# Experts' stage: PE in written order, sum products two chunks later, end and survey of a group in parts

## The chip, the cores and the metric

The kernel runs on one core of a Trainium2 chip. The metric is the device time of one execution in microseconds; lower is better. Five engines work side by side: TensorE (PE, with its weight loads shown apart as PEld), VectorE (DVE), ScalarE (ACT), GpSimd (POOL) and SyncE (SP, which here only issues transfers). Everything is computed in float32.

## The reference

Two layers work on 8192 tokens (32 sequences of 256) of width 128, each a residual step on a layer norm:

```
x = x + causal_attention(layernorm(x))          # 16 heads
x = x + experts(layernorm(x))                   # this case
x = x + hyperbolic_attention(layernorm(x))      # 16 heads, arccosh distances
x = x + feed_forward(layernorm(x))              # 128 -> 512 -> 128
```

The experts' step, cut to its core:

```
topk_idx, topk_weight = gate(x)                 # sigmoid scores, best 2 of 4 groups, best 4 of 16 experts
g = einsum('th,eih->eti', x, gate_proj)         # 16 experts, inner width 64
u = einsum('th,eih->eti', x, up_proj)
expert_out = einsum('eti,ehi->eth', silu(g) * u, down_proj)
y = sum over the 4 chosen experts of topk_weight * expert_out
y = y + (silu(x @ shared_gate.T) * (x @ shared_up.T)) @ shared_down.T
```

## The kernel before

The tokens are cut into 16 groups of 512 (`NG`, `GT`); x of all groups stays on the chip in `self.xg`. The stages follow one another: causal attention, experts, a test of a flag on the chip, and then one of two versions of the second attention with the feed-forward step (here the far one, `far_attention`).

Every expert is computed for every token, and the routing weight, zero for those not chosen, is multiplied in. Two experts of inner width 64 make a chunk of 128 rows, so there are 8 chunks and, as ninth, the shared expert (64 rows): `NCH = 8`. In `experts` the loop goes over groups, and in it over the nine chunks. One chunk is:

- PE: `g_ps` (L696) and `u_ps` (L698), weights times the 512 normed tokens `bxT`;
- ACT: `act`, the Silu of `g_ps` (L700);
- DVE: `act` times `u_ps` (L701), and but for the shared expert times the routing weights `wb` (L703);
- PE: `y_ps`, added up over the nine chunks (L704).

At chunk 1 `fetched` (L671, L677) issues on SP the transfers of the next group's tokens and routing weights. At the end of a group ACT copies the sum to `yT` (L708), and `add_transposed` turns it back with four PE transposes (L109) and adds it to x on DVE (L110).

Then `survey` prepares the second attention for the group: DVE's statistics (L612, L613), POOL's `sxn`, x less its mean (L614), four PE transposes into `xc_ps` (L620), ACT's copy `sxc` (L622), an SP write of it to memory (L623), twice two products `sqk` with the query and key weights (L628), ACT's squares (L633), DVE's sums (L634), and on DVE the end: least and greatest norm, and `ra` (L637 to L642). `survey_result` makes the flag from all groups' ends.

Beside this the routing of the last four groups (12 to 15) is still to be computed: `preparation` returns 26 pieces. In order they are four statistics, deviations, for each group normed (POOL `rxn`, L504), tokens (PE transposes L511) and scored (PE `logits` L520), then `best_groups` (DVE, L541 to L559), and for each group `weights` (DVE comparisons, L533 to L538, and L569 to L574) and `turned` (PE transposes `wT_ps`, L579, and a write to memory). One piece is written out after each odd chunk. The fetch of group 12, at group 11, reads what they write.

No order is fixed by hand in this stage: a planner goes over the program when it is built, with estimated costs, and puts each engine's instructions in a fixed order, by readiness and the order in which they were written. It may take a later one first. In the causal attention before it, `tc.manual_schedule(engines={mybir.EngineType.PE})` keeps PE in the written order while the planner orders the others. [...] `act` has three buffers.

Of the kernel before, what the change touches and what calls it, by code (L numbers as in the profile page):

```python
# [9 lines left out]
F32 = mybir.dt.float32  # L10
BF16 = mybir.dt.bfloat16
AF = mybir.ActivationFunctionType
ALU = mybir.AluOpType
AX = mybir.AxisListType
PSUM = bass.MemoryType.PSUM

P = 128
B, N, D = 32, 256, 128
T = B * N
TG = 4  # L20
GT = TG * P
NG = T // GT
QUAD = 4
EPS = 1e-5

H = 16
DH = D // H
# [4 lines left out]
NE, INTER = 16, 64  # L32
# [8 lines left out]
class Net:  # L41
# [562 lines left out]

    def survey(self, pool, psum, g):

        nc = self.nc
        mv = pool.tile([P, TG, 2], F32, tag="smv", name=f"smv{g}")
        xn = pool.tile([P, TG, D], F32, tag="sxn", bufs=1, name=f"sxn{g}")
        for t in range(TG):  # L610
            st = pool.tile([P, nc.vector.BN_STATS_DIM], F32, tag="sst", bufs=4, name=f"sst{g}_{t}")
            nc.vector.bn_stats(st, self.xg[g][:, t, :])  # L612
            nc.vector.bn_aggr(mv[:, t, :], st)  # L613
            nc.gpsimd.tensor_scalar(xn[:, t, :], self.xg[g][:, t, :], mv[:, t, 0:1], None, ALU.subtract)  # L614
        rv = self.rv[:, g]
        nc.vector.tensor_scalar(rv, mv[:, :, 1], EPS, None, ALU.add)
        nc.vector.reciprocal(rv, rv)
        ps = psum.tile([P, GT], F32, tag="w", name=f"xc_ps{g}")
        for t in range(TG):
            nc.tensor.transpose(ps[:, t * P : (t + 1) * P], xn[:, t, :], self.ident)  # L620
        xc = pool.tile([P, GT], F32, tag="sxc", name=f"sxc{g}")
        nc.scalar.copy(xc, ps)  # L622
        nc.sync.dma_start(out=self.xc[g], in_=xc)  # L623
        n2 = pool.tile([P, TG, 2 * H], F32, tag="sn2", name=f"sn2_{g}")
        for i in range(2):
            qk = psum.tile([P, 2, 2 * D], F32, tag="w", name=f"sqk{g}_{i}")
            for t in range(2):
                nc.tensor.matmul(  # L628
                    qk[:, t], xc[:, (2 * i + t) * P : (2 * i + t + 1) * P], self.w_qkv[:, 0 : 2 * D],
                    start=True, stop=True,  # L630
                )
            sq = pool.tile([P, 2, 2 * D], F32, tag="ssq", bufs=1, name=f"ssq{g}_{i}")
            nc.scalar.activation(sq, qk, AF.Square)  # L633
            nc.vector.tensor_reduce(  # L634
                n2[:, 2 * i : 2 * i + 2], sq.rearrange("p t (h d) -> p t h d", d=DH), AX.X, ALU.add
            )
        nc.vector.tensor_mul(n2, n2, rv.unsqueeze(2).to_broadcast([P, TG, 2 * H]))  # L637
        nc.vector.tensor_reduce(self.ends[:, 0, g : g + 1], n2, AX.XY, ALU.min)
        nc.vector.tensor_reduce(self.ends[:, 1, g : g + 1], n2, AX.XY, ALU.max)
        ra = self.ra[:, g].rearrange("p t s h -> p t (s h)")  # L640
        nc.vector.tensor_scalar(ra, n2, -1.0, 1.0, ALU.mult, ALU.add)
        nc.vector.reciprocal(ra, ra)  # L642

    def survey_result(self, pool, psum):

# [12 lines left out]
    def experts(self, prep):  # L658
        nc, tc = self.nc, self.tc
        NCH = NE * INTER // P  # L660
        w_g, w_u, w_d, s_g, s_u, s_d = (self.w_e[n] for n in ("w_g", "w_u", "w_d", "s_g", "s_u", "s_d"))
        with (
            tc.tile_pool(name="mo", bufs=2) as pool,
            tc.tile_pool(name="mops", bufs=2, space=PSUM) as psum,
        ):

            def fetched(g):


                xT = pool.tile([P, GT], F32, tag="xT", bufs=3, name=f"bxT{g}")  # L670
                nc.sync.dma_start(out=xT, in_=self.xt[g])  # L671
                wb = pool.tile([P, NCH, GT], F32, tag="wb", bufs=3, name=f"wb{g}")
                rows = self.rows[g].rearrange("(c e) t -> e c t", e=2)
                for c in range(0, NCH, 1 if g == 0 else NCH):
                    cs = slice(c, c + 1 if g == 0 else NCH)
                    for e in range(2):
                        nc.sync.dma_start(  # L677
                            out=wb[e * INTER : (e + 1) * INTER, cs], in_=rows[e, cs].partition_broadcast(INTER)
                        )
                return xT, wb  # L680

            pieces = self.preparation(NG // QUAD - 1, prep, psum, "w")
            ready = fetched(0)
            for g in range(NG):
                xT, wb = ready
                y_ps = psum.tile([P, GT], F32, tag="y", name=f"y_ps{g}")
                for c in range(NCH + 1):
                    if c == 1 and g + 1 < NG:
                        ready = fetched(g + 1)
                    shared = c == NCH  # L690
                    m = INTER if shared else P
                    wg = s_g if shared else w_g[:, c * P : (c + 1) * P]
                    wu = s_u if shared else w_u[:, c * P : (c + 1) * P]
                    wd = s_d if shared else w_d[:, c, :]
                    g_ps = psum.tile([P, GT], F32, tag="g", name=f"g_ps{g}_{c}")
                    nc.tensor.matmul(g_ps[:m, :], wg, xT, start=True, stop=True)  # L696
                    u_ps = psum.tile([P, GT], F32, tag="u", name=f"u_ps{g}_{c}")
                    nc.tensor.matmul(u_ps[:m, :], wu, xT, start=True, stop=True)  # L698
                    act = pool.tile([P, GT], F32, tag="act", bufs=3, name=f"act{g}_{c}")
                    nc.scalar.activation(act[:m, :], g_ps[:m, :], AF.Silu)  # L700
                    nc.vector.tensor_mul(act[:m, :], u_ps[:m, :], act[:m, :])  # L701
                    if not shared:
                        nc.vector.tensor_mul(act, act, wb[:, c])  # L703
                    nc.tensor.matmul(y_ps, wd, act[:m, :], start=c == 0, stop=shared)  # L704
                    if c % 2 == 1 and pieces:
                        pieces.pop(0)()
                yT = pool.tile([P, GT], F32, tag="yT", name=f"yT{g}")
                nc.scalar.copy(yT, y_ps)  # L708
                self.add_transposed(pool, psum, "u", g, yT)
                self.survey(pool, psum, g)  # L710
            self.survey_result(pool, psum)


# [785 lines left out]
```

## Time and profile before

| what | value |
|---|---|
| median of 3 runs | 2361.95 us (2359.27 to 2363.54) |
| the profiled execution | 2362.43 us, its span 2360.5 us |
| PE busy | 2084.4 us, 88% of the span |
| DVE busy | 1569.7 us, 67% |
| ACT busy | 1391.4 us, 59% |
| POOL busy | 736.7 us, 31% |
| experts' stage, first g_ps to last yT | 1040.62 to 1507.08 us |
| from there to the flag | 1521.65 us |

Times in the profile are microseconds from the start of the span. A line of a timeline gives start, duration, engine, line of the kernel, operation, what is written and read with its shape, the number of instructions merged, and in brackets the engine's idle time before it with what ended it. The product of 128x512 in float32 is two passes on PE and shows as x2. PE's passes overlap, and their ends are modelled, so lengths are read from start to start.

### The profile page before, as it was taken

Reading aid. Unit: us, or ns where it says so; the run is one execution under the profiler, and the core shown is the slowest. Engines: PE = TensorE matmul, PEld = TensorE weight load, DVE = VectorE, ACT = ScalarE, POOL = GpSimd, SP = SyncE. Lnnn points to the kernel's source line nnn. Section 1 sums busy time; section 2 is a strip of 40 time slices with the busy share of each in tenths; the row PEclk is TensorE's granted clock in tenths of the full one; section 3 lists DMA queues with packets and bytes.
Section 4 is the critical chain, followed back from the end, with each engine's and each line's share of the span. In section 5 each row is a group of like instructions: output and inputs, shape, how many; then the busy total and the mean of one; then the engine's idle time right before and its main releaser. Section 6 shows DMA issues by size and latency. Waiting matters only on the chain.

```text
span 2360.5 us, 38340 instructions
## 1 busy us (share of the span) xinstructions
PE 2084.4 (88%) x14083; PEld 1320.4 (56%) x14083; DVE 1569.7 (67%) x4820; ACT 1391.4 (59%) x2429; POOL 736.7 (31%) x809
## 2 busy tenths in 40 slices
PE   5999999999999999979999999766787787787877
PEld 4777777777777777744443333344444444444443
DVE  2656666587658765765695555457777777777774
ACT  1776677666766676632222222267767777777774
POOL 3000001100010001002110000157777777777773
PEclk9999999999999999989999999878989999999999
DMA  4000000000000000036444332000000000000000
GB/s 145 1 1 2 1 1 6 10 7 3 1 15 6 3 1 14 7 85 135 98 91 90 89 90 49 27 5 5 10 10 14 10 10 14 10 14 10 10 5 20
DMA packets 43940, 66.65 MB, mean 28 GB/s; under 512 B 3616, under 2 KB 16688, under 8 KB 43744
## 3 DMA queue, kind: packets, MB, share of 16 engines
q1 hardware_dynamic: 40960, 59.00, 10.3%
q0 software_dynamic: 1200, 3.78, 0.5%
q8 instruction: 114, 1.87, 0.3%
q10 hardware_dynamic: 1584, 1.34, 0.2%
q14 instruction: 82, 0.67, 0.1%
HBM read 50.99 MB, written 13.11 MB: 27 GB/s over the span
## 4 chain that ended last, share of the span: by engine, by line
PE 57%; DVE 16%; POOL 10%; ACT 8%; issue 6%; DMA 1%; POOLq 0%; ACTq 0%; DVEq 0%; SPq 0%
PE t_ps L258 9%; PE s L286 9%; POOL fv L1192 8%; DVE fv L1184 6%; PE y_ps L704 5%; ACT ft L1177 5%; PE s L279 4%; PE g_ps L696 4%; PE fs L1123 4%; PE av L335 4%; PE u_ps L698 3%; PE pa_ps L316 2%; DVE fxn L1219 2%; PE pb_ps L322 2%; PE pa_ps L315 2%
## 5 line engine op out<-in xcount | busy, mean ns | idle before, releaser
L1192 POOL TENSOR_TENSOR fv<-ft,fv 128x512 f32<-128x512 f32 x480 | 567.4, 1214 | 197.2 <-ACT fv L1187 168.0
L273 DVE CUSTOM_DVE_ANT_0 p<-s,mask 128x128 f32<-128x128 f32 (+1 forms) x1024 | 316.0, 353 | 297.5 <-PE s L279 175.9
L301 ACT ACTIVATE p<-p,lo 128x128 f32<-128x128 f32 (+1 forms) x1024 | 373.7, 444 | 162.9 <-DVE lo L295 162.6
L1184 DVE SCALAR_TENSOR_TENSOR fv<-fs,ft 128x1024 f32<-128x1024 f32 x256 | 301.4, 1219 | 94.7 <-ACT ft L1177 67.8
L1177 ACT ACTIVATE ft<-fs 128x1024 f32<-128x1024 f32 x256 | 248.1, 1021 | 179.6 <-PE fs L1123 169.1
L1123 PE MATMUL fs<-fqT,fkT 32*128 32x256 f32 x2048 | 162.7, 435 | 133.7 <-DVE fv L1184 133.5
L286 PE MATMUL s<-xT,tT 128*128 128x256 f32 x1024 | 266.8, 383 | 9.0 <-DVE lo L273 9.0
L258 PE MATMUL t_ps<-xT,m_all 128*128 128x512 f32 x512 | 252.6, 613 | 3.3 <-ACT score L525 1.9
L1187 ACT ACTIVATE fv<-fv 128x2048 f32<-128x2048 f32 x128 | 246.9, 1929 | 0.0
L700 ACT ACTIVATE act<-g_ps 128x512 f32<-128x512 f32 x144 | 85.9, 596 | 232.4 <-PE g_ps L696 216.1
L1123 PEld LDWEIGHTS fs<-fqT,fkT 32*128 32x128 f32 x2048 | 103.1, 201 | 200.3 <-DVE fv L1184 111.7
L216 POOL TENSOR_TENSOR x<-x,w_bp 128x512 f32<-128x512 f32 x16 | 21.6, 1348 | 613.7 <-DVE xn L213 613.7
L286 PEld LDWEIGHTS s<-xT,tT 128*128 128x128 f32 x1024 | 177.7, 194 | 25.2 <-DVE lo L273 11.6
L259 ACT ACTIVATE tT<-t_ps,m_bias 128x512 f32<-128x512 f32 x256 | 161.0, 672 | 21.0 <-PE t_ps L258 20.6
L504 POOL TENSOR_SCALAR rxn<-x,rmv,rrstd 128x128 f32<-128x128 f32 x64 | 51.2, 811 | 377.3 <-PE rxT_ps L511 223.2
L279 PEld LDWEIGHTS s<-xT,tT 128*128 128x128 f32 x1024 | 134.3, 192 | 60.3 <-issue 56.9
L614 POOL TENSOR_SCALAR sxn<-x,smv 128x128 f32<-128x128 f32 x64 | 44.8, 716 | 384.2 <-DVE smv L613 287.5
L701 DVE TENSOR_TENSOR act<-u_ps,act 128x512 f32<-128x512 f32 x144 | 97.7, 680 | 96.7 <-PE u_ps L698 88.5
L1135 PE MATMUL fav<-fv,fva 128*32 128x257 f32 x2048 | 149.8, 408 | 7.0 <-ACT fqT L1329 2.1
L696 PE MATMUL g_ps<-bxT,w_w_g 128*128 128x512 f32 x256 | 132.9, 604 | 3.1 <-DMA bxT<-xt 3.1
L704 PE MATMUL y_ps<-act,w_w_d 128*128 128x512 f32 x256 | 134.0, 615 | 1.4 <-DVE act L703 0.5
L279 PE MATMUL s<-xT,tT 128*128 128x128 f32 x1024 | 134.9, 275 | 0.0
(223 smaller groups left out, 3736.5 us busy)
## 6 DMA issues: line engine op xcount, KB each, us to landing
wb<-rows SPq DMA_DIRECT2D x30, 1024.0 KB, 8.0
xt<-rxT SPq DMA_DIRECT2D x16, 256.0 KB, 2.0
bxT<-xt SPq DMA_DIRECT2D x16, 256.0 KB, 7.6
xc<-sxc SPq DMA_DIRECT2D x16, 256.0 KB, 2.1
fxc<-xc SPq DMA_DIRECT2D x16, 256.0 KB, 2.6
out<-x SPq DMA_DIRECT2D x16, 256.0 KB, 2.3
x<-in_x SPq DMA_DIRECT2D x8, 256.0 KB, 10.7
x<-in_x POOLq DMA_DIRECT2D x8, 256.0 KB, 10.4
```

What stands on the lines that cost most here:

```text
L258: nc.tensor.matmul(ps, m_all[:, h], G["xT"], start=True, stop=True)
L273: nc.vector.tensor_tensor_reduce(out=out, in0=x, in1=m, scale=-scale, scalar=3e38, op0=ALU.add, op1=ALU.min, accum_out=accum)
L279: nc.tensor.matmul(s0[:, j], tT[:, j, o : o + P], xT[:, o : o + P], start=True, stop=True)
L286: nc.tensor.matmul(s[:, l], tT[:, j + l, o + P : o + N], xT[:, o : o + N], start=True, stop=True)
L301: nc.scalar.activation(p[:, l], p[:, l], AF.Exp, bias=lo[:, c, l : l + 1], scale=-1.0)
L696: nc.tensor.matmul(g_ps[:m, :], wg, xT, start=True, stop=True)
L704: nc.tensor.matmul(y_ps, wd, act[:m, :], start=c == 0, stop=shared)
L1123: nc.tensor.matmul(sc[:, j, kc], kT[rows, kc * P : (kc + 1) * P], qT[rows], start=True, stop=True)
L1177: nc.scalar.activation(t[:, i : i + 2], sc[:, i : i + 2], AF.Relu, scale=-4.0)
L1184: nc.vector.scalar_tensor_tensor(v[:, x, :, 0:N], sc[:, x], 0.5, t[:, x], ALU.subtract, ALU.mult)
L1187: nc.scalar.activation(v[:, :, :, 0:N], v[:, :, :, 0:N], AF.Sqrt, scale=-4.0)
L1192: eng.tensor_sub(v[:, j, :, 0:N], t[:, j], v[:, j, :, 0:N])
```

## The change

PE keeps the written order in the experts' stage. A chunk is now a function `hidden` that issues `g_ps`, `u_ps`, Silu and the products on DVE and returns `add`, which issues the chunk's `y_ps` and, for the shared expert, the copy to `yT`. The loop holds two such functions back, so `y_ps` of chunk c is written after `g_ps` and `u_ps` of chunk c + 2; those of the last two chunks follow chunks 0 and 1 of the next group. `act` has four buffers.

`survey` returns five parts and `finish` puts `add_transposed` ahead of the first. They are written in the next group: yT's transposes, addition, statistics and sxn after chunk 2, the transposes into `xc_ps` after chunk 4, the products `sqk` after chunks 5 and 6, the end after chunk 7. The routing pieces come after chunks 1, 3 and 8: three to a group, where there were four. `add_transposed` takes a bank of tag `w`, where it took `u`. After the last group everything that is left follows at once.

```
     def survey(self, pool, psum, g):
...
+        def centred():
+            mv = pool.tile([P, TG, 2], F32, tag="smv", name=f"smv{g}")
...
+        def turned():
+            ps = psum.tile([P, GT], F32, tag="w", name=f"xc_ps{g}")
+            for t in range(TG):
+                nc.tensor.transpose(ps[:, t * P : (t + 1) * P], made["xn"][:, t, :], self.ident)
+            xc = made["xc"] = pool.tile([P, GT], F32, tag="sxc", name=f"sxc{g}")
+            nc.scalar.copy(xc, ps)
+            nc.sync.dma_start(out=self.xc[g], in_=xc)
+
+        def product(i):
...
+        def ends():
...
+        return [centred, turned, lambda: product(0), lambda: product(1), ends]
...
+            def hidden(g, c, xT, wb):
+
+                shared = c == NCH
...
+                g_ps = psum.tile([P, GT], F32, tag="g", name=f"g_ps{g}_{c}")
+                nc.tensor.matmul(g_ps[:m, :], wg, xT, start=True, stop=True)
+                u_ps = psum.tile([P, GT], F32, tag="u", name=f"u_ps{g}_{c}")
+                nc.tensor.matmul(u_ps[:m, :], wu, xT, start=True, stop=True)
+                act = pool.tile([P, GT], F32, tag="act", bufs=4, name=f"act{g}_{c}")
+                nc.scalar.activation(act[:m, :], g_ps[:m, :], AF.Silu)
+                nc.vector.tensor_mul(act[:m, :], u_ps[:m, :], act[:m, :])
+                if not shared:
+                    nc.vector.tensor_mul(act, act, wb[:, c])
+
+                def add():
+                    if c == 0:
+                        sums[g] = psum.tile([P, GT], F32, tag="y", name=f"y_ps{g}")
+                    nc.tensor.matmul(sums[g], wd, act[:m, :], start=c == 0, stop=shared)
+                    if shared:
+                        yT = sums[g, "T"] = pool.tile([P, GT], F32, tag="yT", name=f"yT{g}")
+                        nc.scalar.copy(yT, sums[g])
+
+                return add
+
+            def finish(g):
+
+                first, *others = self.survey(pool, psum, g)
+
+                def added():
+                    self.add_transposed(pool, psum, "w", g, sums[g, "T"])
+                    first()
+
+                return [added, *others]
+
+            sums, waiting, rest = {}, [], []
             pieces = self.preparation(NG // QUAD - 1, prep, psum, "w")
             ready = fetched(0)
-            for g in range(NG):
...
-                    act = pool.tile([P, GT], F32, tag="act", bufs=3, name=f"act{g}_{c}")
...
-                    nc.tensor.matmul(y_ps, wd, act[:m, :], start=c == 0, stop=shared)
-                    if c % 2 == 1 and pieces:
-                        pieces.pop(0)()
-                yT = pool.tile([P, GT], F32, tag="yT", name=f"yT{g}")
-                nc.scalar.copy(yT, y_ps)
-                self.add_transposed(pool, psum, "u", g, yT)
-                self.survey(pool, psum, g)
+            with tc.manual_schedule(engines={mybir.EngineType.PE}):
+                for g in range(NG):
+                    xT, wb = ready
+                    for c in range(NCH + 1):
+                        if c == 1 and g + 1 < NG:
+                            ready = fetched(g + 1)
+                        waiting.append(hidden(g, c, xT, wb))
+                        if len(waiting) > 2:
+                            waiting.pop(0)()
+
+                        if c == 2 and g:
+                            rest = finish(g - 1)
+                        if c in (2, 4, 5, 6, 7) and rest:
+                            rest.pop(0)()
+                        elif c in (1, 3, 8) and pieces:
+                            pieces.pop(0)()
+                for f in waiting + finish(NG - 1):
+                    f()
             self.survey_result(pool, psum)
```

More of the change, by code (lines that the diff above doesn't have):

```diff
@@ L607, in survey @@
         nc = self.nc
[L608 to L614, printed above, removed]
-        rv = self.rv[:, g]
[L616 to L625, printed above, removed]
+        rv = self.rv[:, g]
+        made = {}
+        def centred():
+            mv = pool.tile([P, TG, 2], F32, tag="smv", name=f"smv{g}")
+            xn = made["xn"] = pool.tile([P, TG, D], F32, tag="sxn", bufs=1, name=f"sxn{g}")
+            for t in range(TG):
+                st = pool.tile([P, nc.vector.BN_STATS_DIM], F32, tag="sst", bufs=4, name=f"sst{g}_{t}")
+                nc.vector.bn_stats(st, self.xg[g][:, t, :])
+                nc.vector.bn_aggr(mv[:, t, :], st)
+                nc.gpsimd.tensor_scalar(xn[:, t, :], self.xg[g][:, t, :], mv[:, t, 0:1], None, ALU.subtract)
+            nc.vector.tensor_scalar(rv, mv[:, :, 1], EPS, None, ALU.add)
+            nc.vector.reciprocal(rv, rv)
+        def turned():
+            ps = psum.tile([P, GT], F32, tag="w", name=f"xc_ps{g}")
+            for t in range(TG):
+                nc.tensor.transpose(ps[:, t * P : (t + 1) * P], made["xn"][:, t, :], self.ident)
[3 more added lines that the diff above has]
+        def product(i):
+            if i == 0:
+                made["n2"] = pool.tile([P, TG, 2 * H], F32, tag="sn2", name=f"sn2_{g}")
             qk = psum.tile([P, 2, 2 * D], F32, tag="w", name=f"sqk{g}_{i}")
@@ L628, in survey @@
                 nc.tensor.matmul(
-                    qk[:, t], xc[:, (2 * i + t) * P : (2 * i + t + 1) * P], self.w_qkv[:, 0 : 2 * D],
+                    qk[:, t], made["xc"][:, (2 * i + t) * P : (2 * i + t + 1) * P], self.w_qkv[:, 0 : 2 * D],
                     start=True, stop=True,
@@ L634, in survey @@
             nc.vector.tensor_reduce(
-                n2[:, 2 * i : 2 * i + 2], sq.rearrange("p t (h d) -> p t h d", d=DH), AX.X, ALU.add
+                made["n2"][:, 2 * i : 2 * i + 2], sq.rearrange("p t (h d) -> p t h d", d=DH), AX.X, ALU.add
             )
[L637 to L642, printed above, removed]
+        def ends():
+            n2 = made["n2"]
+            nc.vector.tensor_mul(n2, n2, rv.unsqueeze(2).to_broadcast([P, TG, 2 * H]))
+            nc.vector.tensor_reduce(self.ends[:, 0, g : g + 1], n2, AX.XY, ALU.min)
+            nc.vector.tensor_reduce(self.ends[:, 1, g : g + 1], n2, AX.XY, ALU.max)
+            ra = self.ra[:, g].rearrange("p t s h -> p t (s h)")
+            nc.vector.tensor_scalar(ra, n2, -1.0, 1.0, ALU.mult, ALU.add)
+            nc.vector.reciprocal(ra, ra)
+        return [centred, turned, lambda: product(0), lambda: product(1), ends]
     def survey_result(self, pool, psum):
@@ L680, in fetched @@
                 return xT, wb
+            def hidden(g, c, xT, wb):
+                shared = c == NCH
+                m = INTER if shared else P
+                wg = s_g if shared else w_g[:, c * P : (c + 1) * P]
+                wu = s_u if shared else w_u[:, c * P : (c + 1) * P]
+                wd = s_d if shared else w_d[:, c, :]
+                g_ps = psum.tile([P, GT], F32, tag="g", name=f"g_ps{g}_{c}")
[15 more added lines that the diff above has]
+                return add
@@ L682, in experts @@
+            def finish(g):
[5 more added lines that the diff above has]
+            sums, waiting, rest = {}, [], []
             pieces = self.preparation(NG // QUAD - 1, prep, psum, "w")
             ready = fetched(0)
-            for g in range(NG):
[L685 to L698, printed above, removed]
-                    act = pool.tile([P, GT], F32, tag="act", bufs=3, name=f"act{g}_{c}")
[L700 to L704, printed above, removed]
-                    if c % 2 == 1 and pieces:
-                        pieces.pop(0)()
-                yT = pool.tile([P, GT], F32, tag="yT", name=f"yT{g}")
-                nc.scalar.copy(yT, y_ps)
-                self.add_transposed(pool, psum, "u", g, yT)
-                self.survey(pool, psum, g)
```

## The prediction, made before the changed kernel had run

> **What bounds it now.** The profiled execution took 2362.43 us: a span of 2360.5 and 1.9 around it. It lies 0.5 above the median of the runs, 2361.95, so a saving in the trace is taken off the median. On the page, PE is the busiest engine and the chain of what ended last lies 57% on it. The change touches one stage, so I cut the span into stretches: the experts run from PE's first g_ps at 1040.62 to the last yT copy at 1507.08. The stretch table gives length, then busy time of PE, weight load, DVE, ACT, POOL, the granted clock and the DMA share:
>
> ```profile
> 1158.50:1190.00 31.50, 30.47 (x84) 13.31 (x83) 26.84 (x60) 8.56 (x15) 2.81 (x4) 1.00 0.41 91
> 1190.00:1221.00 31.00, 28.82 (x79) 12.13 (x78) 28.71 (x58) 8.56 (x15) 3.35 (x4) 1.00 0.39 85
> ...
> 1247.90:1276.70 28.80, 27.78 (x71) 11.45 (x72) 16.57 (x35) 7.72 (x14) 2.70 (x4) 1.00 0.42 91
> ```
>
> In the third row PE is the bound (27.8 of 28.8), DVE has 12 us to spare, the clock is full. In the first two, where the last routing pieces run, DVE has 2 to 5 us left. The period of one group, from the timeline of ACT:
>
> ```profile
> 1391.88 0.58 ACT L708 COPY yT<-y_ps 128x512 f32<-128x512 f32 x1 [2.38 <-PE y_ps L704]
> 1420.68 0.58 ACT L708 COPY yT<-y_ps 128x512 f32<-128x512 f32 x1 [2.38 <-PE y_ps L704]
> ```
>
> It is 28.80, the same for all nine groups from 1247.87 on. A busy PE is not a full one: I laid the starts of one group's products side by side (PE's timeline, with weight loads).
>
> ```profile
> 1451.63 1.02 PE L696 MATMUL g_ps<-bxT,w_w_g 128*128 128x512 f32 x2
> 1453.11 0.33 PE L620 MATMUL xc_ps<-ident,sxn 128*128 128x128 f32 x1 [0.45 <-POOL sxn L614]
> ...
> 1454.62 0.33 PE L620 MATMUL xc_ps<-ident,sxn 128*128 128x128 f32 x1 [0.22 <-POOL sxn L614]
> 1455.20 0.33 PE L620 MATMUL xc_ps<-ident,sxn 128*128 128x128 f32 x1 [0.25 <-POOL sxn L614]
> ...
> 1462.33 1.02 PE L696 MATMUL g_ps<-bxT,w_w_g 128*128 128x512 f32 x2
> ...
> 1463.44 0.30 PEld L704 LDWEIGHTS y_ps<-act,w_w_d 128*128 128x128 f32 x2 [0.92 <-DVE act L703]
> 1463.44 1.13 PE L704 MATMUL y_ps<-act,w_w_d 128*128 128x512 f32 x2
> ...
> 1464.41 1.02 PE L698 MATMUL u_ps<-bxT,w_w_u 128*128 128x512 f32 x2
> ```
>
> A product (two passes) without a wait takes 0.858 from start to start (1460.61, 1461.47, 1462.33). The reader is to see the larger steps: 1.48 before the first survey transpose, 1.11 before y_ps at 1463.44. Summed from 1449.38 to 1478.17: 27 products x 0.858 = 23.15, 8 transposes in two fours of 0.44 = 0.88, eight passes of sqk 1.81, together 25.84. The other 2.95: survey transposes waiting for POOL's sxn 1.47 (0.62 + 0.38 + 0.47); y_ps waiting for act, and the weight load that then starts only with its product, 0.62; steps between tiles of other shapes around the shared expert (128*64, 64*128) 0.65; yT and sqk waiting for a copy, 0.2.
>
> [...] These steps remain after the change, so I take the row: 26.5. [...]
>
> **The change, part by part.**
>
> 1. *Sums two chunks later.* No instruction is added. A chunk of PE is 2.57 (three products), so act has 5.1 where it needs about 1.9 (Silu 0.60, two products on DVE 0.69 each, less the overlap with u_ps). The 0.62 goes; act gets a fourth buffer, so nothing new waits for its release: 0.62 saved per group.
>
> 2. *End and survey in parts.* yT's transposes go to chunk 2 of the next group, sxn's to chunk 4, sqk to 5 and 6. The copy behind yT and the copy behind sxc have a chunk or more, so the 0.2 goes. The tight one is chunk 2 to 4. Now:
>
> ```profile
> 1450.97 0.69 DVE L110 TENSOR_TENSOR x<-y_ps,x 128x512 f32<-128x512 f32 x1 [2.85 <-PE y_ps L109]
> 1452.45 2.70 POOL L614 TENSOR_SCALAR sxn<-x,smv 128x128 f32<-128x128 f32 x4 [26.10 <-DVE smv L613]
> ```
>
> From the addition at 1450.97 to the last transpose at 1455.20 are 4.23. In the new order DVE still has chunk 2's two products before it, some 0.3 after the transposes end, so 4.5 are needed; between stand six products, 5.14. It fits with 0.6, and the 1.47 goes. If the cover is gone, PE waits by the excess. The SP writes of xc follow the copies and the fetches of g+1 stay at chunk 1: SP waits for nothing late (its share of DMA is 0.42).
>
> 3. *PE in the written order.* It costs nothing where inputs are there. Behind a PE instruction that waits, all of PE now waits. The case that matters is wT_ps, which needs the long routing comparisons on DVE (weights). From DVE's timeline:
>
> ```profile
> 1180.49 1.22 DVE L533 TENSOR_TENSOR gte<-choice 128x1024 f32<-128x1024 f32 x1
> ...
> 1188.56 0.21 DVE L569 SCALAR_TENSOR_TENSOR wt<-rank,score 128x64 f32<-128x64 f32 x1
> ```
>
> Five comparisons with four chunk products between, 8.1 us. Start to start, weights is about 6.3, best_groups 3.9, a group's 17 products 0.60 each = 10.2, its survey 5.1. Pieces come three per group now (chunks 1, 3, 8; 26 pieces, to group 8), so the last logits are in group 5's chunk 3 and the first wT_ps in group 6's chunk 3: DVE has 25.5 to do in PE's 26.5, after 1 us of start and with gaps between dependent operations. I put 2 us of PE wait there, 0 to 1 at each of the next two, and 1 at the last (chunk 8 to chunk 3: 6.3 + 4.8 + 2.5 = 13.6 in 11, less what is done ahead): 4. Three survey chains under these comparisons pass their cover by about 1 each (POOL takes 3.35 there instead of 2.70, second row): 3. Both costs are unseen before; bounds 0 and 19 (each of four wT_ps waiting 4, each chain 1). I take 7, near the low end, since DVE's load fits on average: over these three groups 3 x 15.3 + 3.9 + 4 x 6.3 = 75 us, in PE's 3 x 26.5 + 4 x 0.44 = 81.
>
> [...]
>
> 4. *Pieces.* PE's own part is unchanged: rxT_ps 0.44, logits 0.89, wT_ps 0.44, times four = 7.1. Now groups 1 to 6 are 181.3 (1066.57 to 1247.87) against 6 x 28.8 = 172.8, so 8.5 more, 1.4 beyond PE's part.
>
> 5. *Ends of the stage.* Group 0 starts as now (g, u, g, u, g, u, y is already the order from 1040.62). After the last group end and survey follow one another as they do from 1507.08 to 1521.65 (flag): 14.6, no cover before or after. Nothing.
>
> **Sum.** Fifteen group periods end at 1507.08, from 1066.57: 440.5. After: 15 x 26.5 + 7.1 + 7 = 411.6. Saved 28.9, so 2361.95 - 28.9 = **2333**.
>
> **Rivals.**
>
> *A. Half of it is given back* (0.22). DVE comes late in the routing groups and the survey chain doesn't quite fit in quiet ones. For: only 0.6 of slack, and DVE's order is fixed by a plan of costs. With 0.5 per group in 15 groups and 15 instead of 7: 34.5 gross less 7.5, less 13.6 = 13 saved, 2349.
>
> *B. Slower* (0.10). The place is the survey's transposes in chunk 4. If DVE's queue has the addition and statistics behind the products of chunk 3 (their end 3.3 after yT's transposes), the chain is 3.3 + 4.2 = 7.5 against 5.14: 2.4 of PE wait, which eats the 2.3 saved; this is the point from which it decides. Behind chunk 4's as well it is 2.57 more: 15 x 2.6 + 7 = +46, 2400 (half of the groups, 2381). Against: at 1450.97 and 1451.70 DVE did addition and statistics ahead of the next products.
>
> *C. It does nothing* (0.04): the order that PE has is already as good, because DVE, not PE, paces the stage. Against: 16.6 of 28.8 busy in the third row. It gives 2362.
>
> *D. More than forecast* (0.10): shape steps also vanish and no routing wait: 15 x 25.84 + 7.1 = 394.7, 46 saved, 2316.
>
> **How the numbers follow.** The forecast itself has 0.54: 15 periods of 26.3 to 26.8, routing waits of 3 to 14: 2326 to 2343. For 8 in 10 the range takes in A and D's near part: 2319 to 2356. A measurement of this kernel tells 0.2%, some 5 us, from no change. Faster by more: forecast, D and A, 0.85; within: C and the edge of A, 0.05; slower: B, 0.10.
>
> **What would show it.** Right: yT copies 26.3 to 26.8 apart from group 9 on; y_ps weight loads no longer waiting for act; survey transposes without a POOL wait; PE waiting for DVE's wt in groups 6 to 8, some 2 us each. Wrong: a PE wait of over 2 us for sxn in each group (B), periods still near 28.8 with DVE full (C), or granted clock below 1.00 in the stage. All after the flag should be as long as before.

## The result, and the profile after

The changed kernel takes 2328.83 us (median of 4 runs, 2328.09 to 2331.45) against 2362.74 for the kernel before in the same comparison: a ratio of 0.9861, 95% interval 0.9844 to 0.9878, 33.9 us less. Forecast were 2333 and a saving of 28.9, range 2319 to 2356.

The stretches of the changed kernel, one with routing pieces and one quiet group (length, then busy time of PE, weight load, DVE, ACT, POOL, then the granted clock, which is the share of full speed that PE's clock had in the stretch, and the DMA share):

```profile
1207.44:1235.33 27.89, 27.40 (x75) 12.32 (x76) 26.61 (x54) 8.31 (x15) 3.28 (x4) 1.00 0.43 91
1290.01:1316.52 26.51, 26.51 (x71) 12.03 (x71) 16.66 (x36) 7.73 (x13) 2.70 (x4) 1.00 0.46 97
```

The quiet group went from 28.80 to 26.51 with the same instructions, and PE has no gap in it. In the routing group DVE is busy for 26.6 of 27.9, and PE still waits for little (0.5). From ACT's timeline, two yT copies in a row:

```profile
1369.55 0.58 ACT L718 COPY yT<-y_ps 128x512 f32<-128x512 f32 x1 [1.31 <-PE y_ps L715]
1396.06 0.58 ACT L718 COPY yT<-y_ps 128x512 f32<-128x512 f32 x1 [1.31 <-PE y_ps L715]
```

PE's timeline between them, at the place where the survey's transposes waited for POOL before:

```profile
1376.85 1.02 PE L715 MATMUL y_ps<-act,w_w_d 128*128 128x512 f32 x2
1377.71 0.60 PE L626 MATMUL xc_ps<-ident,sxn 128*128 128x128 f32 x4
1378.15 1.02 PE L703 MATMUL g_ps<-bxT,w_w_g 128*128 128x512 f32 x2
```

The four transposes now run as one block of 0.44, where before they came one by one with 1.47 of waiting ahead of them and between. And the weight loads at the end of a group, from PEld's timeline:

```profile
1391.81 0.19 PEld L715 LDWEIGHTS y_ps<-act,w_w_d 128*128 128x128 f32 x1 [0.24 <-issue]
...
1394.90 0.29 PEld L715 LDWEIGHTS y_ps<-act,w_s_d 64*128 64x128 f32 x2 [0.76 <-issue]
1395.95 0.30 PEld L703 LDWEIGHTS g_ps<-bxT,w_w_g 128*128 128x128 f32 x2 [0.76 <-issue]
```

The first starts at 1391.81, its product at 1392.24: the load is drawn ahead. The other two start with their products (1394.90, 1395.96), although the profile names nothing that they waited for (0.76 each, put down to issue). These are the steps around the shared expert, 0.73 in a group, that the change leaves.

Where the 33.5 us of the profiled executions (2360.5 to 2327.0) come from: from the first g_ps to the last yT 466.46 became 432.51, 33.95 less; the stage begins 0.96 earlier; its end, yT to flag, is 0.13 shorter; what follows the flag is 1.5 longer (838.9 to 840.4). Nothing was changed there, and over all runs below it lies between 836.8 and 845.3, while the start of the stage lies between 1033.3 and 1041.1. That is noise as large as some of the effects, so for small differences I use the stage's own length and the steady period, the distance of yT copies in the quiet groups from group 9 on, which repeats to 0.01 in most runs. The stage's length has some noise too: its first group took 30.07 here and 29.12 and 30.47 in two runs below (e1_planner, e10_act3) whose other groups are the same to 0.01. The last sums of a group now stand behind two chunks of the next, so the first group ends 3.4 later and the last period is 3.4 shorter (23.08); the two cancel.

### The profile page after: what moved, and what is told of

Read it like the earlier page. It is cut to its first block, busy times and chain, and to the rows that moved or that the text cites. A ratio compares the mean times of both kernels' runs of the same rounds, so it can differ in the third digit from the quotient of the medians.

```text
span 2327.0 us, 38348 instructions
## 1 busy us (share of the span) xinstructions
PE 2065.8 (89%) x14083; PEld 1329.2 (57%) x14083; DVE 1570.4 (67%) x4820; ACT 1391.8 (60%) x2429; POOL 736.5 (32%) x809
## 4 chain that ended last, share of the span: by engine, by line
PE 62%; DVE 14%; POOL 9%; ACT 7%; issue 5%; DMA 1%; POOLq 0%; ACTq 0%; DVEq 0%; SPq 0%
PE t_ps L258 9%; PE s L286 9%; POOL fv L1234 8%; DVE fv L1226 6%; PE g_ps L703 5%; PE y_ps L715 5%; PE u_ps L705 5%; ACT ft L1219 4%; PE s L279 4%; PE fs L1165 4%; PE av L335 4%; PE pa_ps L316 2%; PE pb_ps L322 2%; PE pa_ps L315 2%; DVE fxn L1261 2%
## 5 line engine op out<-in xcount | busy, mean ns | idle before, releaser
L316 PE MATMUL pa_ps<-ident,p 128*128 128x128 f32 x512 | 131.4, 281 | 2.9 <-ACT p L301 2.9
```

Source lines behind the costliest of these rows:

```text
L316: nc.tensor.transpose(ps[:, l, P:], p1[:, j + l, 0:P], self.ident)
```

## The experiments

Each is the changed kernel with one edit, or with that edit and PE's order left to the planner. Where no range stands with a time, there was one run. Lengths and periods:

| run | PE's order | sums held back | end and survey | steady period | first g_ps to last yT |
|---|---|---|---|---|---|
| kernel before | planner | 0 | at once, at the group's end | 28.80 | 466.5 |
| changed kernel | as written | 2 | parts | 26.51 | 432.5 |
| e1_planner | planner | 2 | parts | 26.51 | 431.6 |
| e5_planner_delay0 | planner | 0 | parts | 27.05 | 440.0 |
| e6_planner_whole | planner | 2 | at once, chunk 2 | 28.28 | 458.2 |
| e2_delay1 | as written | 1 | parts | 26.51 | 437.4 |
| e9_delay0 | as written | 0 | parts | 42.15 | 701.0 |
| e3_whole | as written | 2 | at once, chunk 2 | 34.0 | 541.3 |
| e7_pieces4 | as written | 2 | parts, 4 pieces a group | 26.51 | 442.9 |
| e8_planner_pieces4 | planner | 2 | parts, 4 pieces a group | 26.51 | 435.6 |
| e10_act3 | as written | 2 | parts | 26.51 | 432.9 |
| e4_padded | as written | 2 | parts | 25.78 | 421.1 |
| e11_rows_only | as written | 2 | parts | 26.12 | 427.0 |

### Is it the order by hand? (e1_planner)

```
-            with tc.manual_schedule(engines={mybir.EngineType.PE}):
+            with ExitStack():
```

> The changed kernel without the fixed order of PE; positions in the program, delays and parts stay. Theory (what counts is where the work is written, because then nearly every input is there and the planner finds no reason to go another way): within 5 us of the changed kernel, 2324 to 2334 us, steady period 26.5. Rival (the order by hand is what makes the gain): the planner draws survey transposes and sums forward to where it believes them ready, PE waits for POOL and act again, steady period 27.5 to 28.8, 2345 us or more.

Measured: 2325.83 us (2324.38 to 2329.68), ratio to the kernel before 0.9862 (0.983 to 0.989); the period is 26.51, and the list of the 15 periods is that of the changed kernel to within 0.01. The fixed order is worth nothing here. The gain lies in where the work is written.

### Which part brings what (e5_planner_delay0, e6_planner_whole)

Both leave PE's order to the planner, as e1_planner does, and take one of the two moves back. First the sums:

```
-                        if len(waiting) > 2:
+                        if len(waiting) > 0:
```

> The planner orders PE, the sums follow their own chunk as in the kernel before; only the end and survey in parts is kept. If the parts of the 2.3 us per group add up as the prediction put them: y_ps waits for act again (0.62), the survey and copy waits stay away (1.47 + 0.2), steady period 26.5 + 0.6 = 27.1, some 9 us above the changed kernel, 2333 to 2341 us. Rival (with a free chunk to fill, the planner finds work for PE and the sums' place is worth nothing): 26.5. Rival (it is the sums that matter, and the survey waits only took their place): 28 or more.

Measured: 2334.05 us (2331.78 to 2337.34), period 27.05, stage 7.5 longer than in the changed kernel. From PEld's timeline in a quiet group of this run:

```profile
1400.10 0.30 PEld L715 LDWEIGHTS y_ps<-act,w_w_d 128*128 128x128 f32 x2 [0.69 <-DVE act L710]
1401.82 0.30 PEld L715 LDWEIGHTS y_ps<-act,w_w_d 128*128 128x128 f32 x2 [0.56 <-DVE act L710]
```

The loads of y_ps wait for act again, by 0.69 and 0.56; in the kernel before, such a load started with its product (both at 1463.44). Then the parts:

```
                             rest = finish(g - 1)
+                            while rest:
+                                rest.pop(0)()
```

> The planner orders PE, the sums come two chunks later, the whole end and survey is written at chunk 2 of the next group. If the parts add up: the survey transposes are drawn forward and wait for POOL again (1.47) and sqk for its copy (0.1 to 0.2), steady period 26.5 + 1.6 = 28.1, some 24 us above the changed kernel, 2348 to 2356 us, against 2434 with PE in the written order. Rival (with the sums' inputs long ready, the planner fills the waits of the chain with them): 26.5 to 27.

Measured, with the planner: 2351.02 us (2347.51 to 2356.26), ratio 0.9966 (0.9958 to 0.9973), period 28.28, stage 25.7 longer. The waits of PE and of its loads between 1280 and 1450 us, some six groups (us in total, times, the longest):

```profile
PE xc_ps L626 <- POOL sxn L619: 6.1, 18, 0.6
PEld xc_ps L626 <- POOL sxn L619: 17.0, 24, 1.4
```

It is the wait for POOL that is back. So of the 2.29 per group, the parts alone bring 1.75 (28.80 to 27.05), the sums alone 0.52 (28.80 to 28.28), together 2.27: they add up. One reserve: survey and end stand at chunk 2 in the second, at the end of their own group in the kernel before. Another: both runs keep the other bank of `add_transposed`, which no run takes back alone.

### How far back a sum must be (e2_delay1, e9_delay0)

```
-                        if len(waiting) > 2:
+                        if len(waiting) > 1:
```

> The changed kernel with one chunk held back instead of two. From the start of u_ps to act being ready the trace of the changed kernel shows 1391.38 to 1393.92, 2.54; with one chunk held back four products of 0.858 lie between, 3.43. Theory: it fits where DVE is free and fails by some tenths only where the statistics, the end of the survey or the routing comparisons stand ahead on DVE: 0 to 0.8 in a group, 2329 to 2341 us. Rival (two chunks are what takes the wait away): the 0.62 per group comes back and more, in every group, 2340 us or more.

Measured: 2333.78 us (2329.22 to 2336.16); quiet groups stay at 26.51, the stage is 4.9 longer. Some 1.7 of it come at the start, where the first y_ps waits 1.45 for act (1041.62), and 2.5 in the one group that takes 30.22 instead of 27.73, where DVE computes routing weights. There PE's steps at y_ps, which waits for act, are 0.9 longer in three places, and 1.5 are the survey's:

```profile
1244.46 0.33 PE L626 MATMUL xc_ps<-ident,sxn 128*128 128x128 f32 x1 [1.71 <-POOL sxn L619]
```

The changed kernel waits 0.22 at this place. So the first chunk takes away the wait in quiet groups. The second is a reserve for the start and for a busy DVE, but of less than the 2.5; why the survey's chain comes later with one chunk is left open.

> The changed kernel with no sum held back: PE in the written order, each y_ps right after its own u_ps. From the start of u_ps to act being ready are 2.54, one product of 0.858 lies between, so PE waits some 1.7 and then pays a weight load, 1.8 in each of 144 chunks: +260, 2580 to 2600 us, more where DVE is busy; no wait is long enough to lower the clock (the 2.2 us gaps of the run with the whole survey are, so the clock is the doubt). Rival (the sums' place is worth no more than the 0.5 per group that it is worth under the planner): under 2345 us.

Measured: 2594.07 us, period 42.15, so 15.6 more over nine chunks, 1.74 each. One chunk in PE's timeline:

```profile
1403.58 1.02 PE L703 MATMUL g_ps<-bxT,w_w_g 128*128 128x512 f32 x2
1404.44 1.02 PE L705 MATMUL u_ps<-bxT,w_w_u 128*128 128x512 f32 x2
1407.04 1.13 PE L715 MATMUL y_ps<-act,w_w_d 128*128 128x512 f32 x2 [1.58 <-DVE act L710]
```

The same sums at their own chunk cost 0.5 per group with the planner, which fills the wait, and 15.6 with PE in the written order. The granted clock was 0.97 from 1300 to 1500. It fell to 0.50 for 3.41 in a quiet group, behind a wait of 1.72 (the last section shows it). The expectation had no wait long enough for that.

### The survey at once, PE in the written order (e3_whole)

Its edit is that of e6_planner_whole, with PE's order fixed.

> The changed kernel with the whole end and survey of a group written at chunk 2 of the next, PE in the written order. Theory (parts are what covers the chain): PE waits from the transposes of yT to the last one of sxn, some 4.5, and for the copy behind it 0.7, so about 5.2 in each of 15 groups: +78, 2400 to 2415 us. Rival (the chain is hidden anyway, or PE's time is bound by something else): under 2345 us.

Measured: 2434.33 us, 105.5 above the changed kernel and not 78; quiet periods of 33.6 to 34.1. PE's timeline:

```profile
1380.66 0.60 PE L109 MATMUL y_ps<-ident,yT 128*128 128x128 f32 x4
1383.53 0.33 PE L626 MATMUL xc_ps<-ident,sxn 128*128 128x128 f32 x1 [2.27 <-POOL sxn L619]
...
1386.42 3.78 PE L636 MATMUL sqk<-w_w_qkv,sxc 128*128 128x256 f32 x8 [0.68 <-ACT sxc L628]
1389.99 1.64 PE L703 MATMUL g_ps<-bxT,w_w_g 128*128 128x512 f32 x2
1391.46 1.02 PE L705 MATMUL u_ps<-bxT,w_w_u 128*128 128x512 f32 x2
```

From 1380.66 to 1386.42 are 5.76, of which the eight transposes need 0.88: 4.9 of waiting. Then sqk takes 3.57 instead of 1.72 and the next product 1.47 instead of 0.86: another 2.5, with the granted clock at 0.70 from 1380.66 to 1389.99. Together 7.3, as this group's period shows (33.85). The expectation had the wait and left out the clock.

### Routing pieces closer together (e7_pieces4, e8_planner_pieces4)

```
-                        elif c in (1, 3, 8) and pieces:
+                        elif c in (0, 1, 3, 8) and pieces:
```

> The changed kernel with four routing pieces to a group (chunks 0, 1, 3, 8) instead of three. Theory (PE in the written order waits at wT_ps when DVE has more to do than PE between two pieces): DVE needs some 25.8 from the logits to the first weights (trace of the changed kernel, 1185.62 to 1211.45), PE's way is now eight chunks with the survey, some 24.3; the second and fourth wT_ps come two chunks after the one before, 5.1, where weights with its chunk products need 8.7. Waits of about 1.5 + 3.5 + 0 + 3 = 8 us in groups 4 to 6, 2331 to 2340 us, no change in other periods. Rival (DVE's backlog isn't seen by PE): within 2 us of the changed kernel.

Measured: 2331.97 us; stage 10.4 longer. Nearly all of the wait is at one place, the second wT_ps:

```profile
1174.81 1.12 PE L715 MATMUL y_ps<-act,w_s_d 64*128 64x512 f32 x2
1184.08 1.01 PE L579 MATMUL wT_ps<-ident,wt 128*16 128x128 f32 x4 [8.14 <-DVE wt L574]
1184.89 1.91 PE L703 MATMUL g_ps<-bxT,w_w_g 128*128 128x512 f32 x2
1186.59 1.91 PE L705 MATMUL u_ps<-bxT,w_w_u 128*128 128x512 f32 x2
```

The sum came out about right (8.1 of wait), but by luck, since its spread was wrong: the first, third and fourth wT_ps don't wait. DVE's timeline tells why the second waits so long:

```profile
1178.67 0.21 DVE L569 SCALAR_TENSOR_TENSOR wt<-rank,score 128x64 f32<-128x64 f32 x1
1178.81 1.21 DVE L533 TENSOR_TENSOR gte<-choice 128x1024 f32<-128x1024 f32 x1
1179.94 0.20 DVE L571 TENSOR_REDUCE tot<-wt 128x4 f32<-128x64 f32 x1
1180.07 1.21 DVE L535 TENSOR_TENSOR eqe<-choice 128x1024 f32<-128x1024 f32 x1
...
1183.72 0.22 DVE L574 SCALAR_TENSOR_TENSOR wt<-wt,tot 128x64 f32<-128x64 f32 x1
```

Between the short last steps of one group's weights the planner put the long comparisons of the next group's, four of 1.2. What PE waits for comes 5.3 after 1178.67, though its own steps are under 1 us; the next group's weights are ready early for it. And after the wait three products run at 1.70, 1.71 and 1.19 instead of 0.86: 2.0 more, the clock again (granted 0.58 from 1177 to 1188 and 0.88 from 1188 to 1192).

> The same four pieces to a group, with the planner ordering PE. Theory (the fixed order is worth nothing where inputs are there, and costs where they are late): the planner goes round the late wT_ps, the waits shrink to 0 to 3 us, 2323 to 2332 us. Rival (the wait is DVE's load, whatever the order of PE): as with the fixed order.

Measured: 2328.23 us; stage 3.1 longer than in the changed kernel. None of PE's waits is at wT_ps; 2.5 are the survey's transposes waiting for POOL, where the changed kernel has 0.7. So the fixed order gained nothing in these runs where inputs are there, and where one is late it accounts for 7.3 of the 10.4.

### The fourth buffer (e10_act3)

```
-                act = pool.tile([P, GT], F32, tag="act", bufs=4, name=f"act{g}_{c}")
+                act = pool.tile([P, GT], F32, tag="act", bufs=3, name=f"act{g}_{c}")
```

> The changed kernel with three buffers for act, as before, instead of four. Silu of chunk c writes where act of c - 3 was, whose y_ps stands before g_ps of chunk c on PE: the buffer is free when it is wanted. Theory: nothing, steady period 26.51. Rival (with sums two chunks later a third buffer is still held): Silu waits for y_ps, steady period over 27.

Measured: 2325.12 us, period 26.51. The fourth buffer brings nothing here.

### The steps that remain (e4_padded, e11_rows_only)

```
-        self.w_e = {n: self.load(keep, n, eng) for n in ("w_g", "w_u", "w_d", "s_g", "s_u", "s_d")}
+        self.w_e = {n: self.load(keep, n, eng) for n in ("w_g", "w_u", "w_d")}
+        for n in ("s_g", "s_u", "s_d"):
+            t = self.w_e[n] = keep.tile([P, P], F32, name=f"w_{n}")
+            self.nc.gpsimd.memset(t, 0.0)
+            rows, cols = self.w[n].shape
+            eng.dma_start(out=t[:rows, :cols], in_=self.w[n])
...
-                m = INTER if shared else P
+                m = P
```

> The changed kernel with the shared expert's three weights padded with zeros to 128 columns or rows, so that its products have the same shape as the others (the zero rows add nothing to the sum). Theory (the steps around the shared expert, 0.65 a group, come from the change of shape): steady period 25.85 to 26.0, 16 groups save 8 to 10.5 us, 2318 to 2321 us. Rival (a weight load is drawn ahead whatever its shape, and the steps come from something else): within 2 us of the changed kernel.

Measured: 2314.08 us (2311.80 to 2322.73), ratio to the kernel before 0.9807 (0.9783 to 0.9831), 11.75 below e1_planner, which was measured beside it; period 25.78, stage 11.4 shorter than in the changed kernel, a little more than expected. PE's timeline across the shared expert's last product:

```profile
1385.67 1.02 PE L710 MATMUL u_ps<-bxT,w_w_u 128*128 128x512 f32 x2
1386.53 1.02 PE L720 MATMUL y_ps<-act,w_s_d 128*128 128x512 f32 x2
1387.38 1.02 PE L708 MATMUL g_ps<-bxT,w_w_g 128*128 128x512 f32 x2
```

0.86 and 0.85, where the changed kernel has 0.95 and 1.06. The zero rows cost no PE time: with the steps gone, the padded product takes 0.85, as the others do. This is the fastest version of the study.

```
+        t = self.w_e["s_d"] = keep.tile([P, D], F32, name="w_s_d")
+        self.nc.gpsimd.memset(t, 0.0)
+        eng.dma_start(out=t[:INTER], in_=self.w["s_d"])
+        self.last = [keep.tile([P, GT], F32, name=f"last{i}") for i in range(2)]
...
-                act = pool.tile([P, GT], F32, tag="act", bufs=4, name=f"act{g}_{c}")
+                act = self.last[g % 2] if shared else pool.tile([P, GT], F32, tag="act", bufs=4, name=f"act{g}_{c}")
...
-                    nc.tensor.matmul(sums[g], wd, act[:m, :], start=c == 0, stop=shared)
+                    nc.tensor.matmul(sums[g], wd, act, start=c == 0, stop=shared)
```

> The changed kernel with only the shared expert's last product padded to 128 rows (weights and act with zeros below row 64); its g_ps and u_ps stay 64 columns wide. The steps of the changed kernel around the 64-row product are 0.09 before, 0.20 and 0.10 behind, 0.39; around the two of 64 columns 0.10, 0.05, 0.09 and 0.10, 0.34. If each shape costs its own steps, the steady period is 26.51 - 0.39 = 26.12; if only the row count matters, 25.78; if only the column count matters, 26.51.

Measured: 2321.73 us, period 26.12, the first of the three cases expected: rows cost 0.39 and columns 0.34 a group, each its own.

## Why the prediction was right, and where it was off

**The ledger of a quiet group** held in every line to about a tenth. Forecast 26.5, measured 26.51. It had 1.47 for POOL and 0.2 for the copies, together 1.67: the parts alone bring 1.75. It had 0.62 for act: the sums alone bring 0.52, the sums on top of the parts 0.54. It had 0.65 for the shapes that stay: padding takes away 0.73. That it met 26.51 to 0.01 is luck: sqk, entered with 1.81, takes 1.72 without its wait, and that makes up for the 0.08 of the shapes.

**The steps around the shared expert**, the row that the forecast took, are these starts in PE's timeline of the kernel before:

```profile
1474.21 1.07 PE L696 MATMUL g_ps<-bxT,w_s_g 128*64 128x512 f32 x2
1475.12 1.02 PE L698 MATMUL u_ps<-bxT,w_s_u 128*64 128x512 f32 x2
1476.07 1.12 PE L704 MATMUL y_ps<-act,w_w_d 128*128 128x512 f32 x2
1477.12 1.12 PE L704 MATMUL y_ps<-act,w_s_d 64*128 64x512 f32 x2
1478.17 1.13 PE L696 MATMUL g_ps<-bxT,w_w_g 128*128 128x512 f32 x2
```

The steps are 0.91, 0.95, 1.05 and 1.05, where a product takes 0.858; without such steps the forecast would have had 25.84 for a group. To take them over was right: in the changed kernel the loads at 1394.90 and 1395.95 still start with their products. e4_padded shows what they hang on here: with all products of one shape the steps around the shared expert's last product are 0.86 and 0.85, and the group takes 25.78. Rival D, which had the shape steps vanish, didn't come about by the change, but by an edit of a few lines on top of it.

**The tight chain from chunk 2 to 4** was placed to a tenth: the addition starts 0.32 after yT's transposes end (1399.07 to 1399.39, forecast 0.3), and of the 5.14 of cover 0.67 was left (POOL ends at 1403.55, the transposes start at 1404.22; forecast 0.6):

```profile
1399.39 0.68 DVE L110 TENSOR_TENSOR x<-y_ps,x 128x512 f32<-128x512 f32 x1
1400.85 2.70 POOL L619 TENSOR_SCALAR sxn<-x,smv 128x128 f32<-128x128 f32 x4 [23.81 <-DVE smv L618]
1404.22 0.60 PE L626 MATMUL xc_ps<-ident,sxn 128*128 128x128 f32 x4
```

Rival B had DVE's queue put chunk 3's products ahead of the addition. It didn't. (B's 2400 and 2381 leave out the 7 of its own sum: 2408 and 2388. The upper end of the forecast's own part is 2344.5, not 2343. Neither moves the forecast.)

**The wrong term: the routing waits, step 3.** Forecast were 4 us of wait for wT_ps and 3 for the survey chains. The group periods 2 to 8 of the changed kernel lie 8.2 above steady, of which PE's own pieces are 7.1; the waits are some 1 us. All that the trace shows of them is 0.7, and it belongs to the survey's chain:

```profile
1216.66 0.33 PE L626 MATMUL xc_ps<-ident,sxn 128*128 128x128 f32 x1 [0.24 <-POOL sxn L619]
1217.24 0.33 PE L626 MATMUL xc_ps<-ident,sxn 128*128 128x128 f32 x1 [0.25 <-POOL sxn L619]
...
1244.54 0.33 PE L626 MATMUL xc_ps<-ident,sxn 128*128 128x128 f32 x1 [0.22 <-POOL sxn L619]
```

No wT_ps waits, though PE waiting for wt was named as a sign of being right. From DVE's and PE's timelines, at the place where 2 us were put:

```profile
1186.88 0.29 DVE L541 TENSOR_SCALAR score<-score 128x256 f32<-128x256 f32 x1 [0.32 <-ACT score L525]
...
1211.23 0.22 DVE L574 SCALAR_TENSOR_TENSOR wt<-wt,tot 128x64 f32<-128x64 f32 x1
```

```profile
1185.62 0.96 PE L520 MATMUL logits<-w_gate_w,rxT 128*128 128x16 f32 x8
...
1213.03 0.60 PE L579 MATMUL wT_ps<-ident,wt 128*16 128x128 f32 x4
```

DVE began 1.3 after logits and took 24.6 (forecast 1 and 25.5, and gaps), PE's way was 27.4 with its own pieces in it (forecast 26.5), so wT_ps found its weights 1.6 early (1211.45 to 1213.03). The last wT_ps, where 1 us was put, runs at 1268.64; its weights were finished at 1257.3. The load fitted, and I charged waits for a queue that is nearly full on average but wasn't behind at any of the four places where PE wants its weights. The mechanism exists, as e7_pieces4 shows: four pieces to a group are enough for a wait of 8.1. With the term at 1 instead of 7 the forecast would have been 2327. The stage was forecast to get 28.9 shorter and got 33.95 shorter: 5.9 from this term, less 0.7 in group 0 (three products at a granted clock of 0.50, 1039.66 to 1044.91, instead of two) and 0.15 from the periods.

**PE in the written order** was put at nothing where inputs are there. That holds. e1_planner shows that it is worth nothing either, and e8_planner_pieces4 that it costs where an input is late; the forecast didn't ask what it brings. Rival A (half given back) would have needed what e7_pieces4 does. Rival C is out: PE paced the stage, and in the quiet groups it now does so without a gap.

**The clock** has no term in the forecast's sum. The only low stretch of the stage is its start, in both kernels. In the kernel before:

```profile
1040.62 2.00 PE L696 MATMUL g_ps<-bxT,w_w_g 128*128 128x512 f32 x2 [3.08 <-DMA bxT<-xt]
1042.41 1.86 PE L698 MATMUL u_ps<-bxT,w_w_u 128*128 128x512 f32 x2
1044.10 1.02 PE L696 MATMUL g_ps<-bxT,w_w_g 128*128 128x512 f32 x2
```

Behind 3.08 without work the first two products take 3.48 instead of 1.72, at a granted clock of 0.51; from 1044.10 to 1507 it is 1.00. In the changed kernel the wait is 3.24, and the first three products run at 0.50. From there on (1044.91 to 1473) the clock is 1.00; no wait of PE, from the stage's second product to the last yT, is longer than 0.25.

## What to carry to other kernels

Lay the starts of one period's instructions on the busiest engine side by side and sum what they need: what is left over is the gain to be had, and each piece of it has a cause that one can name and price. Move a consumer in the program to where its input is long ready, rather than fixing an order: then a planner has no reason to leave it, while a fixed order turns each late input into a standstill. A queue that is nine tenths full needs a comparison at each place where it is waited for (when is it ready, when is it wanted); a flat charge for being full was some seven times too high here.

## What the runs showed of the hardware

In the changed kernel the weight loads at the changes of shape around the shared expert start with their products: the 128x64 load at 1387.69 (product 1387.70), the 64x128 load at 1394.90 (1394.90), the 128x128 loads behind them at 1389.56 and 1395.95 (1389.56 and 1395.96). That makes 0.05 to 0.20 per step, 0.73 per group for three products of 64 rows or columns. Not every change of shape did it: the first 128x16 load of wT_ps, behind one of 128x128, starts at 1212.60 and its product at 1213.03. Padding with zeros to the common shape cost PE nothing here and was worth 11.4 us.

The clock fell in sparse work too, not only in a long gap. In e7_pieces4 the two products soon after a wait of 8.14 took 1.70 and 1.71, twice their time. But in e3_whole no wait of PE between 1300 and 1550 was longer than 2.3, with transposes in between, and the eight passes of sqk behind them still took 3.57 instead of 1.72. In e9_delay0, where the gaps lie between full products, the clock fell behind a wait of 1.72, in a quiet group. PE's timeline and the stretch after it, with the granted clock (0.50) third from the end:

```profile
1474.49 1.12 PE L715 MATMUL y_ps<-act,w_w_d 128*128 128x512 f32 x2 [1.72 <-DVE act L710]
1475.55 1.76 PE L703 MATMUL g_ps<-bxT,w_s_g 128*64 128x512 f32 x2
1477.09 1.91 PE L705 MATMUL u_ps<-bxT,w_s_u 128*64 128x512 f32 x2
```

```profile
1475.80:1479.21 3.41, 3.21 (x4) 0.46 (x2) 0.10 (x1) 0.59 (x1) 0.00 (x0) 0.50 1.00 226
```

And in the second attention of the changed kernel the same sixteen products took 2.09 behind a wait of 2.65, at a granted clock of 0.50, but 1.15 behind one of 2.68, at 1.00:

```profile
1520.05 2.09 PE L1165 MATMUL fs<-fqT,fkT 32*128 32x256 f32 x16 [2.65 <-DVE fv L1226]
...
1544.61 1.15 PE L1165 MATMUL fs<-fqT,fkT 32*128 32x256 f32 x16 [2.68 <-DVE fv L1226]
```

So the length of the gap just before doesn't decide alone; what does was not shown.
